# Two queues for the first four row tiles, and two inner products in rotating PSUM tiles

## The chip, the cores and the metric

The kernel runs on one core of one Trainium2 chip. The metric is the device time of one execution in microseconds. Before the change it is 921.42 us, the median of three runs (920.85 to 922.02).

## The reference

One decoder layer with three sublayers, each followed by a layer norm without weights, all in float32. x is 16 x 256 tokens of 256 channels; the context has the same shape.

```python
# 1. "attention" against fixed keys and values, 4 heads of 64
xn = layernorm(x) * ln_g + ln_b
s  = einsum('bhtd,sd->bhts', heads(xn), w_fc.reshape(-1, 64))
a  = einsum('bhts,sd->bhtd', square(relu(s)), w_proj.T.reshape(-1, 64))
x  = LN(x + (x + a))
# 2. cross attention, 16 heads of 16, with a bias from clipped differences of frac
attn = gamma * (Q @ K.T) / 4 + delta * (ap * max(D, 0) + an * min(D, 0))
x  = LN(x + softmax(attn) @ V @ Wo.T + bo)
# 3. feed forward with one of 8 experts, chosen by argmax(x @ gate_W.T + gate_b)
h  = relu(x @ wi_W.T + wi_b + lora_e(x))          # 1024 wide, lora of rank 4
x  = LN(x + h @ wo_W.T + wo_b)
```

## The kernel before

The 4,096 tokens are cut into eight blocks of 512, and each block into four row tiles of 128 tokens by 256 channels. The work has three stages, one after the other, with their edges overlapped. In the first, the fixed attention goes block by block: a block's rows are normalized, turned by TensorE, multiplied with the keys `kT` (L314), put through a relu on ACT (L322) and a square on DVE (L324), and multiplied with the values `vv` (L334). In the second, the cross attention goes through 64 groups of four heads, and the feed forward of blocks 0 to 6 is worked in between them. In the third, a tail, what is left of block six and all of block seven's feed forward are done. The order on each engine is the order in which the code is written (`manual_schedule`); nothing is reordered. Every engine takes its own queue in order: arithmetic, waits and the issues of transfers alike.

The start. Block 0 is loaded in four pieces, one for each row tile (L263), all issued by SP; then SP issues the two copies of `kT` (`load_first`, L83), one for each half of the partitions, then the whole of block 1 (L260), and then the weights of the cross attention (`load_cross`, L113: `wk`, `wv`, `wq`, then small vectors, L115 and L120). ACT issues the columns `ln_g` and `ln_b` (L70), loads its function table (L78) and issues `vv` (L84). Block 0's `begin` then takes mean and variance of each row tile on DVE as it comes (L189, L190), the inverse root by `ln` and `exp` on ACT (L198, L200) and three small steps on DVE, and normalizes; `turn_in` transposes and applies `ln_g` and `ln_b`; the scores follow.

Transfers that SP and ACT issue share eight completion semaphores, which the tile layer hands out in turn, in the order in which it takes the transfers to be issued. An issue whose semaphore was used by an earlier transfer waits on its queue until that one has landed.

The tail. `inner(half)` multiplies a block with four of the eight column tiles of `wi` (L828), one into each of the four PSUM tiles `banks[0..3]`; `lora(half)` adds the expert's product (L840) and empties the four through a relu into `hT`, banks 0 and 2 on ACT (L847), banks 1 and 3 on DVE (L851). `finish(j)` multiplies a row tile of `hT`, all eight column tiles in order, with `wof` (L858) into a rotating tile and adds the result to the rows on DVE (L871). Rotating tiles come from `tile_b` (L49): two buffers of one pool and, as every third, one of another, so three in turn. A tile is handed out again only when its last reader is done.

In the tail, block six goes: `inner(0)`, `lora(0)`, `inner(1)` (L1152), the last batch's output projection `project` (L559), `lora(1)`, `finish(0)`, `finish(1)`; then block seven's `turn` and block six's `finish(2)`. The changed lines are in these functions:

Of the kernel before, what the change touches and what calls it, by code (L numbers as in the profile page):

```python
# [9 lines left out]
FP = mybir.dt.float32  # L10
AF = mybir.ActivationFunctionType
ALU = mybir.AluOpType
AX = mybir.AxisListType

P = 128
# [6 lines left out]
def tile_decoder_layer(ctx: ExitStack, tc: tile.TileContext, a: dict, out: bass.AP):  # L22


    nc = tc.nc
# [4 lines left out]
    CC = C // P  # L30
# [9 lines left out]
    const = ctx.enter_context(tc.tile_pool(name="const", bufs=1))  # L40
# [8 lines left out]
    def tile_b():  # L49

        if turns:
            turns[0] += 1
            if turns[0] % 3 == 0:
                return psV.tile([P, 512], FP, tag="W", name="ps_b")
        return psB.tile([P, 512], FP, tag="B", name="ps_b")
# [9 lines left out]
    rev = const.tile([P, 4, E], FP, name="rev")  # L65
    for e in range(E):
        nc.gpsimd.memset(rev[:, :, e : e + 1], float(E - e))
    def columns(name, src, eng):
        t = const.tile([P, src.shape[1]], FP, name=name)
        eng.dma_start(out=t, in_=src)  # L70
        return t


    kT = const.tile([P, 4, C], FP, name="kT")
    ln_g = columns("ln_g", a["ln_g"], nc.scalar)
    ln_b = columns("ln_b", a["ln_b"], nc.scalar)

    nc.scalar.preload_act_table_set("natural_log_exp_and_others")  # L78
    vv = const.tile([P, CC, C], FP, name="vv")

    def load_first():
        for h in range(2):
            nc.sync.dma_start(out=kT[64 * h : 64 * h + 64], in_=a["kT"])  # L83
        nc.scalar.dma_start(out=vv, in_=a["vv"].rearrange("(c p) f -> p c f", p=P))  # L84


# [17 lines left out]
    wib = const.tile([P, FC], FP, name="wib")  # L104
# [3 lines left out]
    loraB = const.tile([P, F], FP, name="loraB")  # L108

    def load_cross():  # L110
        load = nc.sync.dma_start
        for t, n in ((wk, "wkT"), (wv, "wvT"), (wq, "wqT")):
            load(out=t, in_=a[n].rearrange("(c p) f -> p c f", p=P))  # L113
        for t, n in ((bq, "bq"), (bk, "bk"), (fcol, "frac_cols")):
            load(out=t, in_=a[n])  # L115
        for t, n in (
            (bo, "bo"), (apos, "alpha_pos"), (aneg, "alpha_neg"), (gamma, "gamma"),
            (delta, "delta"),
        ):
            load(out=t, in_=a[n].to_broadcast(list(t.shape)))  # L120

        wo_view = a["woT"].rearrange("(o g i d) f -> i g d o f", o=CC, g=4, i=2)
        bv_view = a["bv"].rearrange("x (o g i d) -> i g d (x o)", o=CC, g=4, i=2)
        for i in range(2):
            for g in range(4):
                rows = slice(64 * i + 16 * g, 64 * i + 16 * g + 16)
                load(out=wo[rows], in_=wo_view[i, g])
                load(out=bvc[rows], in_=bv_view[i, g])
# [92 lines left out]
    x_view = a["x"].rearrange("(b j p) c -> b p j c", j=4, p=P)  # L221

    def tile_x():
        return px.tile([P, 4, C], FP, tag="x", bufs=3, name="x")
# [11 lines left out]
    if True:  # L236
# [16 lines left out]
        class Block:  # L253
# [3 lines left out]
            def load(self):  # L257
                self.x = tile_x()
                if self.tb:
                    nc.sync.dma_start(out=self.x, in_=x_view[self.tb])  # L260
                else:
                    for j in range(4):
                        nc.sync.dma_start(out=self.x[:, j, :], in_=x_view[0, :, j, :])  # L263

            def measure(self, jj):
                for j in range(2 * jj, 2 * jj + 2):
# [120 lines left out]
    if True:  # L387

        vaug = []
        for i in range(2):  # L390
            t = const.tile([P, 2, NH, 2 * HD], FP, name=f"vaug{i}")
# [311 lines left out]
        def step(piece):  # L703
            if piece:
                next(piece, None)
# [3 lines left out]
    if True:  # L709
        out_view = out.rearrange("(b j p) c -> b p j c", j=4, p=P)  # L710

        class Block:
# [99 lines left out]
                self.umT = pm.tile([P, 512], FP, tag="umT", bufs=1, name="umT")  # L812
                nc.scalar.copy(self.umT, ps)

            def inner(self, half, gs=range(4)):
                if half == 0 and 0 in gs:
                    if self.tb == NB - 1:
                        h0 = pm.tile([P, 4, 512], FP, tag="pT", name="hT0")
                        h1 = p2.tile([P, 4, 2, S], FP, tag="neg", bufs=3, name="hT1")
                        self.hT = [h0[:, g] for g in range(4)]  # L820
                        self.hT += [h1[:, g].rearrange("p j k -> p (j k)") for g in range(4)]
                    else:
                        h = pm.tile([P, FC, 512], FP, tag="hT", bufs=1, name="hT")
                        self.hT = [h[:, f] for f in range(FC)]
                for g in gs:
                    f = 4 * half + g
                    for c in range(CC):
                        nc.tensor.matmul(  # L828
                            banks[g],
                            lhsT=wi[:, c, f * P : (f + 1) * P],  # L830
                            rhs=self.xT[:, c, :],
                            start=(c == 0),
                            stop=False,
                        )

            def lora(self, half, scalar=(0, 2)):
                for g in range(4):
                    f = 4 * half + g
                    rows = slice(ER * g, ER * g + ER)
                    nc.tensor.matmul(  # L840
                        banks[g], lhsT=loraB[rows, f * P : (f + 1) * P], rhs=self.umT[rows, :],
                        start=False, stop=True,
                    )
                for g in range(4):
                    f = 4 * half + g
                    if g in scalar:
                        nc.scalar.activation(  # L847
                            self.hT[f], banks[g], AF.Relu, bias=wib[:, f : f + 1]
                        )
                    else:  # L850
                        nc.vector.tensor_scalar(  # L851
                            self.hT[f], banks[g], wib[:, f : f + 1], 0.0, ALU.add, ALU.max
                        )

            def outer(self, j, ps):
# [37 lines left out]
    with tc.manual_schedule():  # L893
        rows_in[0].load()
        load_first()
        rows_in[1].load()
        rows_in[0].begin()
# [99 lines left out]
        banks = [psL.tile([P, 512], FP, tag=f"L{g}", name=f"ps_l{g}") for g in range(4)]  # L997
# [11 lines left out]
        six, seven = rows_out[NB - 2 :]  # L1009
# [139 lines left out]
        six.inner(0, range(3, 4))  # L1149
        six.lora(0)  # L1150
        end.divide()
        six.inner(1)  # L1152
        step(add)
        step(add)
        six.lora(1)
# [95 lines left out]
```

## Time and profile before

| | before |
|---|---|
| median of three runs | 921.42 us |
| profiled execution | 922.08 us |
| its span, first to last instruction | 920.2 us |
| TensorE busy | 897.5 us (98%), granted clock 0.997 |
| VectorE busy | 700.7 us (76%) |
| ScalarE busy | 591.9 us (64%) |
| GpSimd busy | 361.6 us (39%) |
| first matmul | 8.90 us |
| first product with `kT` | 11.07 us |

A profile is one execution on the chip, and its times are in microseconds from the span's start. PE is TensorE, PEld its weight load, DVE is VectorE, ACT is ScalarE, POOL is GpSimd, SP is the engine that only issues transfers. SPq and ACTq are the queues in which transfers are issued. A row of the timeline has the start, the duration (of all instructions merged in the row), engine, line, operation, the tile written and the tiles read, and how many instructions there are; in brackets stands how long the engine was idle before and what released it. A busy share is a mean over stages with different limits; what ends last where the change is made decides.

### The profile page before, as it was taken

Reading aid. Unit: us, or ns where it says so; the run is one execution under the profiler, and the core shown is the slowest. Engines: PE = TensorE matmul, PEld = TensorE weight load, DVE = VectorE, ACT = ScalarE, POOL = GpSimd, SP = SyncE. Lnnn points to the kernel's source line nnn. Section 1 sums busy time; section 2 is a strip of 40 time slices with the busy share of each in tenths; the row PEclk is TensorE's granted clock in tenths of the full one; section 3 lists DMA queues with packets and bytes.
Section 4 is the critical chain, followed back from the end, with each engine's and each line's share of the span. In section 5 each row is a group of like instructions: output and inputs, shape, how many; then the busy total and the mean of one; then the engine's idle time right before and its main releaser. Section 6 shows DMA issues by size and latency. Waiting matters only on the chain.

```text
span 920.2 us, 19083 instructions
## 1 busy us (share of the span) xinstructions
PE 897.5 (98%) x6910; PEld 544.7 (59%) x6910; DVE 700.7 (76%) x1972; ACT 591.9 (64%) x990; POOL 361.6 (39%) x352
## 2 busy tenths in 40 slices
PE   5999999999999999999999999999999999999997
PEld 2333333333466666668757766865875686586555
DVE  5798898988869688768777877876787777678443
ACT  4757877778689789646746765675675566566111
POOL 1102312222477567534625553462555346244010
PEclk9999999999999999999999999999999999999999
DMA  5411011100001221110111102011110201111001
GB/s 152 128 36 35 30 39 38 64 2 1 7 6 54 65 72 36 24 46 18 42 36 41 46 17 64 20 42 38 40 44 19 69 14 42 37 29 44 24 1 46
DMA packets 44190, 37.01 MB, mean 40 GB/s; under 512 B 14912, under 2 KB 40000, under 8 KB 44096
## 3 DMA queue, kind: packets, MB, share of 16 engines
q1 hardware_dynamic: 43536, 35.52, 13.9%
q8 instruction: 55, 0.90, 0.4%
q14 instruction: 39, 0.32, 0.1%
q10 hardware_dynamic: 560, 0.26, 0.1%
HBM read 21.07 MB, written 6.03 MB: 29 GB/s over the span
## 4 chain that ended last, share of the span: by engine, by line
PE 58%; ACT 2%; DVE 1%; issue 0%; ACTq 0%; DVEq 0%
PE ps_b L858 12%; PE ps_l L828 12%; PE ps_b L647 10%; PE ps_l L607 6%; PE ps_v L663 5%; PE ps_b L559 3%; PE ps_b L479 2%; PE ps_b L457 2%; PE ps_l L840 2%; PE ps_b L437 1%; ACT ps_l L598 1%; PE ps_b L747 1%; ACT pT L654 1%; PE ps_b L424 1%; PE ps_b L762 0%; ACT qT L447 0%
## 5 line engine op out<-in xcount | busy, mean ns | idle before, releaser
L586 POOL TENSOR_SCALAR neg<-dneg,aneg,delta 128x512 f32<-128x512 f32 x192 | 160.6, 848 | 250.6 <-ACT pT L654 224.3
L622 DVE CUSTOM_DVE_ANT_0 neg<-ps_l,neg 128x256 f32<-128x256 f32 x512 | 181.4, 420 | 47.0 <-PE ps_l L607 46.0
L598 ACT ACTIVATE ps_l<-dpos,apos_d 128x512 f32<-128x512 f32 x256 | 173.1, 687 | 31.7 <-DVE mx L622 29.1
L654 ACT ACTIVATE pT<-ps_b 128x512 f32<-128x512 f32 x256 | 143.4, 591 | 61.1 <-PE ps_b L647 59.5
L324 DVE TENSOR_TENSOR pr<-r 128x1024 f32<-128x1024 f32 x128 | 155.5, 1255 | 32.2 <-ACT r L322 31.9
L322 ACT ACTIVATE r<-ps_a 128x1024 f32<-128x1024 f32 x128 | 126.4, 1022 | 59.0 <-PE ps_a L314 33.4
L647 PE MATMUL ps_b<-ident,neg 128*128 128x128 f32 x1024 | 141.1, 279 | 4.9 <-ACT pT L654 4.0
L637 POOL TENSOR_TENSOR neg<-neg,mx 128x1024 f32<-128x1024 f32 x65 | 123.9, 1907 | 39.8 <-DVE mx L622 33.4
L647 PEld LDWEIGHTS ps_b<-ident,neg 128*128 128x128 f32 x1024 | 113.5, 141 | 43.3 <-issue 16.0
L314 PE MATMUL ps_a<-xnT,kT 64*64 64x512 f32 x1024 | 123.7, 598 | 0.3 <-ACT r L322 0.3
L334 PE MATMUL ps_v<-pr,vv 64*64 64x512 f32 x1024 | 123.5, 593 | 0.3
L858 PE MATMUL ps_b<-wof,hT 128*128 128x256 f32 x512 | 115.9, 381 | 0.1
L828 PE MATMUL ps_l<-xt,wi 128*128 128x512 f32 x256 | 115.0, 596 | 0.8 <-ACT hT L847 0.8
L858 PEld LDWEIGHTS ps_b<-wof,hT 128*128 128x128 f32 x512 | 96.4, 190 | 16.3 <-issue 2.3
L637 DVE TENSOR_TENSOR neg<-neg,mx 128x1024 f32<-128x1024 f32 x63 | 82.5, 1310 | 0.3
L607 PE MATMUL ps_l<-kM,qT 32*128 32x256 f32 x1024 | 78.9, 401 | 1.5 <-DMA kM<-keys 1.0
L334 PEld LDWEIGHTS ps_v<-pr,vv 64*64 64x64 f32 x1024 | 38.1, 132 | 70.7 <-issue 43.7
L349 POOL TENSOR_TENSOR xt<-xt,half 128x512 f32<-128x512 f32 x15 | 23.8, 1587 | 141.1 <-ACT half L348 141.1
L314 PEld LDWEIGHTS ps_a<-xnT,kT 64*64 64x64 f32 x1024 | 37.9, 134 | 67.9 <-issue 56.2
L828 PEld LDWEIGHTS ps_l<-xt,wi 128*128 128x128 f32 x256 | 46.7, 190 | 52.0 <-issue 46.1
L663 PE MATMUL ps_v<-pT,vaug 128*32 128x256 f32 x1024 | 70.5, 388 | 0.8 <-ACT pT L654 0.8
L851 DVE TENSOR_SCALAR hT<-ps_l,wib 128x512 f32<-128x512 f32 x44 | 30.5, 746 | 44.4 <-PE ps_l L840 44.4
(108 smaller groups left out, 977.9 us busy)
## 6 DMA issues: line engine op xcount, KB each, us to landing
cT<-in_ctxT SPq DMA_DIRECT2D x16, 256.0 KB
kM<-keys SPq DMA_DIRECT2D x128, 32.0 KB
v<-raw SPq DMA_DIRECT2D x128, 32.0 KB
invs<-rows SPq DMA_DIRECT2D x128, 32.0 KB
x<-in_x SPq DMA_DIRECT2D x7, 512.0 KB
out<-x SPq DMA_DIRECT2D x7, 512.0 KB
frow<-in_frac SPq DMA_DIRECT2D x16, 128.0 KB
wi<-in_wiT SPq DMA_DIRECT2D x1, 1024.0 KB
```

The costliest lines, as they stand in the source:

```text
L314: nc.tensor.matmul(sc[64 * k : 64 * k + 64, h, :], lhsT=kT[64 * h : 64 * h + 64, q, hf * P + 64 * k : hf * P + 64 * k + 64], rhs=self.xnT[ ...
L324: nc.vector.tensor_tensor(pr, r, r, ALU.mult)
L334: nc.tensor.matmul(self.acc[k][64 * h : 64 * h + 64, :], lhsT=vv[64 * k : 64 * k + 64, hf, 64 * q : 64 * q + 64], rhs=pr[64 * k : 64 * k + ...
L586: nc.gpsimd.tensor_scalar(self.neg[:, g], self.batch.dneg, aneg[:, h : h + 1], delta, ALU.mult, ALU.mult,)
L598: nc.scalar.activation(banks[g], self.batch.dpos.rearrange("p j k -> p (j k)"), AF.Copy, scale=apos_d[:, h : h + 1],)
L607: nc.tensor.matmul(banks[g][:, j * S : (j + 1) * S], lhsT=self.batch.qT[rows, self.o, j * P : (j + 1) * P], rhs=self.batch.kM[rows, self.i ...
L622: nc.vector.tensor_tensor_reduce(out=self.t[:, g, j, :], in0=banks[g][:, j * S : (j + 1) * S], in1=self.neg[:, g, j, :], scale=1.0, scalar ...
L637: eng.tensor_tensor(rows, rows, top.to_broadcast([P, 4, S]), ALU.subtract)
L647: nc.tensor.transpose(ps[:, k * S + j * P : k * S + (j + 1) * P], self.t[:, g, j, k * P : (k + 1) * P], ident,)
L654: nc.scalar.activation(self.pT[:, g, :], self.ps[g], AF.Exp)
L828: nc.tensor.matmul(banks[g], lhsT=wi[:, c, f * P : (f + 1) * P], rhs=self.xT[:, c, :], start=(c == 0), stop=False,)
L858: nc.tensor.matmul(ps[:, 0:C], lhsT=self.hT[f][:, j * P : (j + 1) * P], rhs=wof[:, f, :], start=(f == 0), stop=(f == FC - 1),)
```

## The change

Row tiles 0 and 2 of block 0 are issued by SP, 1 and 3 by ACT. `ln_g`, `ln_b`, the table load, both copies of `kT` and `vv` are issued by ACT, in this order, after its two row tiles; SP goes on with block 1 and the cross attention's weights.

`inner` gets an argument `own`: for the column tiles named there it takes a rotating tile in the place of its bank, and `lora` adds to and empties what `inner` used. Block six's second half is called with `own=(0, 1)`; every other call is as it was.

```diff
-    def columns(name, src, eng):
-        t = const.tile([P, src.shape[1]], FP, name=name)
-        eng.dma_start(out=t, in_=src)
-        return t
-
     kT = const.tile([P, 4, C], FP, name="kT")
-    ln_g = columns("ln_g", a["ln_g"], nc.scalar)
-    ln_b = columns("ln_b", a["ln_b"], nc.scalar)
-
-    nc.scalar.preload_act_table_set("natural_log_exp_and_others")
+    ln_g, ln_b = (const.tile([P, CC], FP, name=n) for n in ("ln_g", "ln_b"))
     vv = const.tile([P, CC, C], FP, name="vv")

     def load_first():
+        for t, n in ((ln_g, "ln_g"), (ln_b, "ln_b")):
+            nc.scalar.dma_start(out=t, in_=a[n])
+
+        nc.scalar.preload_act_table_set("natural_log_exp_and_others")
         for h in range(2):
-            nc.sync.dma_start(out=kT[64 * h : 64 * h + 64], in_=a["kT"])
+            nc.scalar.dma_start(out=kT[64 * h : 64 * h + 64], in_=a["kT"])
         nc.scalar.dma_start(out=vv, in_=a["vv"].rearrange("(c p) f -> p c f", p=P))
...
                     for j in range(4):
-                        nc.sync.dma_start(out=self.x[:, j, :], in_=x_view[0, :, j, :])
+                        eng = nc.scalar if j % 2 else nc.sync
+                        eng.dma_start(out=self.x[:, j, :], in_=x_view[0, :, j, :])
...
-            def inner(self, half, gs=range(4)):
+            def inner(self, half, gs=range(4), own=()):
+
+                if 0 in gs:
+                    self.banks = list(banks)
...
                 for g in gs:
                     f = 4 * half + g
+                    if g in own:
+                        self.banks[g] = tile_b()
                     for c in range(CC):
                         nc.tensor.matmul(
-                            banks[g],
+                            self.banks[g],
...
-                        banks[g], lhsT=loraB[rows, f * P : (f + 1) * P], rhs=self.umT[rows, :],
+                        self.banks[g], lhsT=loraB[rows, f * P : (f + 1) * P], rhs=self.umT[rows, :],
...
-                            self.hT[f], banks[g], AF.Relu, bias=wib[:, f : f + 1]
+                            self.hT[f], self.banks[g], AF.Relu, bias=wib[:, f : f + 1]
...
-                            self.hT[f], banks[g], wib[:, f : f + 1], 0.0, ALU.add, ALU.max
+                            self.hT[f], self.banks[g], wib[:, f : f + 1], 0.0, ALU.add, ALU.max
...
-        six.inner(1)
+        six.inner(1, own=(0, 1))
         step(add)
         step(add)
         six.lora(1)
```

## The prediction

> **What bounds the kernel now.** I read the page's busy table first, then TensorE's share of the steps, then the timeline of the two places that the change touches, the SP queue's own waits, and the DMA rates of the first 20 us. The busy line and the stage table (us; PE, PEld, DVE, ACT, POOL busy; clock, DMA share, GB/s):
>
> ```profile
> PE 897.5 (98%) x6910; PEld 544.7 (59%) x6910; DVE 700.7 (76%) x1972; ACT 591.9 (64%) x990; POOL 361.6 (39%) x352
> ...
> 16.00:40.00 24.00, 24.00 (x224) 8.94 (x220) 19.93 (x27) 17.09 (x23) 1.28 (x1) 1.00 0.51 147
> 40.00:100.00 60.00, 59.97 (x538) 22.67 (x530) 51.22 (x88) 40.62 (x55) 9.85 (x8) 1.00 0.09 28
> ```
>
> TensorE is full from 16 us on (24.00 of 24.00, 59.97 of 60.00). So whatever the start gains or loses reaches the end nearly one for one. The start, from the timeline (start, duration, engine, line):
>
> ```profile
> 0.74 1.81 SPq L263 DMA_DIRECT2D x<-in_x  x4
> ...
> 1.69 0.42 ACTq L84 DMA_DIRECT2D vv<-in_vv  x1
> ...
> 3.84 0.59 SPq L260 DMA_DIRECT2D x<-in_x  x1
> ...
> 4.47 0.51 SPq L113 DMA_DIRECT2D wk<-in_wkT  x1
> ...
> 6.06 0.43 DVE L189 BATCH_NORM_STATS2 st<-x 128x6 f32<-128x256 f32 x1 [0.43 <-DMA x<-in_x]
> ...
> 6.80 0.30 ACT L198 ACTIVATE ln<-mv,epst 128x4 f32<-128x4 f32 x1 [3.87 <-DVE mv L190]
> ...
> 10.86 0.33 SPq L120 DMA_DIRECT2D aneg<-in_alpha_neg  x1
> ...
> 11.07 4.32 PE L314 MATMUL ps_a<-xnT,kT 64*64 64x512 f32 x24
> ```
>
> The last of the four row tiles arrives at 6.06; its statistics free ACT's `ln` at 6.80, and 4.27 us later the first score product starts. The queue's own waits, and GB/s in 40 slices of 0.5 us from zero:
>
> ```profile
> SPq L120 <- DMA x<-in_x: 0.9, 1, 0.9
> ...
> SPq L120 <- DMA wk<-in_wkT: 0.4, 1, 0.4
> ...
> GB/s 0 0 0 68 205 266 152 324 393 387 217 295 209 191 201 309 346 373 369 371 342 269 178 80 30 7 1 23 40 64 7 64 2 66 0 66 19 47 33 33
> ```
>
> An issue can thus be held by the landing of an earlier transfer that it has nothing to do with: a small load (L120) waits for `wk`. The program as built shows why. There are eight completion semaphores, used in turn, and the ninth transfer to be issued waits until the first has landed. `aneg` waits for `wk`'s, so `wk` landed at 10.86.
>
> **The start, what moves.** Row tiles 0 and 2 stay on SP, 1 and 3 go to ACT; `ln_g`, `ln_b`, the table load, the two halves of `kT` and `vv` follow on ACT; on SP the next block's 512 KB and `wk` move up behind two row tiles. The built program's waits on ACT are then: first `kT` for row tile 1, second `kT` for row tile 2, and `vv` for `wk`. `vv` is the third queued instruction ahead of `ln`. ACT's queue runs in order, so `ln` and all that follows stand behind the landing of `wk`, which no arithmetic needs yet.
>
> *Row tiles.* Four issues in one queue took 1.81 us; two and two take half, so the last tile is issued 0.9 us sooner, and neither `vv` nor the tiny `ln` columns share its way. The bounds for the end of the statistics (6.70 before: 6.52 and 0.18): with no wait after the first tile at 2.96, four pairs of 0.56 us give 5.2; with only the issue time saved, 5.8. I take 5.4, since the best slices (393, 387) had both queues on row-sized pieces. Alone that would be 1.3 us gained.
>
> The Trainium skill ("DMA: Bandwidth & Descriptors", section "Issuing engines are not separate DMA queues") says that issuing from several engines saves only the sequencer's time. By it the statistics end at 5.8 and the gain is 0.9 instead of 1.3, if nothing holds `ln`.
>
> *The hold.* When does `wk` land? Before, what had to pass up to and with it was x 524, `vv` 262, `kT` 524, next x 524, `wk` 262 = 2096 thousand bytes. The rate line, half a microsecond a slice, sums to 1968 by 9.0 us and reaches 2096 at 9.35; it landed at 10.86, a lag of 1.5 us. After, `vv` is not ahead (it waits for `wk`). With all of `kT` ahead: 1834, reached at 8.6 in the old rate line, landing 10.1. With none of `kT` ahead: 1310, reached at 6.8, landing 8.3. The old line is slow at first (345 thousand by 3.5 us, one queue issuing); at 390 GB/s from 2.0 the four tiles would be through at 3.35 instead of 4.05, so up to 0.7 us comes off: 9.4 and 7.6. `kT` is issued only after row tile 1, about 3.2, so by the 1.0 us from first issue to first data it starts near 4.3, when most of the next block's rows still have to move; it then shares. Hence between the two, 8.6. The far ends: 6.1, if the lag were gone as well (7.6 less 1.5), and 10.1. Adding `vv`'s own issue (0.42) and 0.03 before `ln`, `ln` starts at 9.05 against 6.80: **+2.25 us** (ends -0.25 and +3.75).
>
> How the two queues share is shown by 4.0 to 4.5 us, where ACT's queue had 69.5% and SP's 41.7% of the engines' time. The skill (same page, "Queues, rings and completion order") has each DMA engine alternate between queues packet by packet. As `kT`'s pieces are the larger, by that rule nearly all of `kT` passes first, 9.4, and the sum would be +3.05.
>
> *Nothing else is late.* `kT` is needed 4.27 us after `ln`, at 13.3, and by the bound above everything up to `kT` has landed by 10.1. `vv` is issued at 8.6 and first needed at 16.6 + 2.25; 262 thousand bytes at the 200 GB/s of the slow slices take 1.3 us, with the lag 2.8. The second block's x lands sooner and is read at step 3. SP's later loads wait on the same ring of semaphores at about the old times, and none is read before the second block's steps. `ln_g`/`ln_b` are issued by 2.6 and read at 12. The table load (1.28) ends near 4, before `ln`.
>
> **The tail, block six.** Before, the second half's first product must wait until ACT has emptied bank 0 (start, duration, engine, line; idle before it):
>
> ```profile
> 855.87 1.14 PE L840 MATMUL ps_l<-umT,loraB 32*128 32x512 f32 x8
> ...
> 857.03 1.27 ACT L847 ACTIVATE hT<-ps_l,wib 128x512 f32<-128x512 f32 x2 [2.19 <-PE ps_l L840]
> ...
> 857.77 7.13 PE L828 MATMUL ps_l<-xt,wi 128*128 128x512 f32 x16 [0.76 <-ACT hT L847]
> ...
> 867.63 7.17 PE L858 MATMUL ps_b<-wof,hT 128*128 128x256 f32 x32
> 867.72 1.27 ACT L847 ACTIVATE hT<-ps_l,wib 128x512 f32<-128x512 f32 x2 [9.42 <-PE ps_l L840]
> ```
>
> Removed: 0.76 us, since two rotating tiles, last read at 846 to 851, are free; banks 2 and 3 are emptied by 858.5, before TensorE comes to them (857.0 + 2 x 1.8 = 860.6). Next in line is `project`: `oT` is ready at 862.71 and TensorE would come at about 863.6, so no stall. But the rotation has three tiles. After the two come `project` (turn_um's old tile) and then `finish(0)`, which gets the tile of the first of the two. In the built program its first product waits for the ACT relu that empties that tile. Before, it started at once (867.63) because it began with the first half's `hT`; the same relu was needed only by its fifth product, behind four others. Now lora ends at 866.94, the relu runs from 866.96 for 0.64 (half of 1.27), and TensorE resumes 0.76 after lora's end, as it did at 857.77. **-0.76 + 0.76 = 0**; ends -0.76 (no new wait) and +0.2 (relu 0.1 late, no full gain). `finish(1)` gets the other tile, emptied by DVE long before, and from there the tiles repeat as before. DVE's earlier work gains nothing: `turn` starts when `finish(1)` ends (874.6).
>
> **The sum.** Span 920.2 + 2.25 + 0 = 922.45. The profiled execution took 922.08, 1.88 around its span, and lies 0.66 above the median of 921.42. Median after: 921.42 + 2.25 = **923.7 us**. 0.2% (1.84 us) is about what a measurement of this kernel can tell from no change.
>
> **Rivals.**
> - *The start gains (not slower).* Were `wk` to land before 6.35, `ln` would not be late. With the hold gone altogether and the statistics at 5.4: 921.42 - 1.3 = 920.1, and 919.4 if the tail also keeps its 0.76. For it: `wk` is issued near 2.2 instead of 4.47. Against: 1310 thousand bytes by 6.35 less the 1.5 lag would need 460 GB/s from 2.0 on; the best slice is 393.
> - *`kT` passes first and the lag grows.* `wk` at 10.1 or a little later: +3.75, 925.2. For it: the slices with `kT` in them (5.0 to 7.5) have only 191 to 295 GB/s. Against: it starts behind the row tiles and finds the next block half moved.
> - *The tail keeps its gain.* If the relu that frees the tile came under other work: 923.7 - 0.76 = 922.9. Against: the wait stands in the built program and nothing lies between lora and `finish(0)`.
>
> **How the numbers follow.** Forecast (+0.5 to +3.3) 0.78, of which about 0.55 above 1.84 and 0.23 under it; start gains 0.09 (0.05 of it faster by over 0.2%, 0.04 within); `kT` first 0.08; tail gains 0.05 (half within). So slower 0.65, same 0.30, faster 0.05. For the forecast alone 921.9 to 924.7; with the rivals and the 0.6 us by which the shown runs differ from their median, 921.0 to 925.4.
>
> **What the profile will show.** Right: `vv`'s issue on ACT's queue near 8.6, `ln` straight behind it near 9.05 with its releaser a DMA or issue rather than `mv`; statistics done near 5.4; first score near 13.3; at the tail no gap before the half's first product, and a gap of about 0.76 with releaser ACT hT before the first product of `finish(0)`. Wrong: `ln` within 0.3 us of the last `mv`, scores before 11, or `kT`/`vv` named as what TensorE waits for.

## The result and the profile after

The changed kernel takes 924.64 us (median of 11 runs, 922.0 to 925.52) against 921.42 us before (11 runs, 919.95 to 922.42). The ratio is 1.0032, with a 95% interval of 1.0021 to 1.0043: slower by 1.9 to 4.0 us. The forecast was 923.7 in a range of 921.0 to 925.4.

Runs of one kernel differ by 1.6 to 4.4 us from the fastest to the slowest. So below, a mechanism is read from the rows of a profile and a verdict from the ratio, never from the span of a single run.

The start of the kernel after, from the timeline (start, duration, engine, line; idle before and its releaser):

```profile
0.73 0.86 SPq L260 DMA_DIRECT2D x<-in_x  x2
0.73 0.89 ACTq L260 DMA_DIRECT2D x<-in_x  x2
...
2.12 0.51 SPq L109 DMA_DIRECT2D wk<-in_wkT  x1
...
3.43 0.43 DVE L185 BATCH_NORM_STATS2 st<-x 128x6 f32<-128x256 f32 x1 [3.43 <-DMA x<-in_x]
3.60 1.17 ACTq L79 DMA_DIRECT2D kT<-in_kT  x2
...
5.05 0.40 DVE L185 BATCH_NORM_STATS2 st<-x 128x6 f32<-128x256 f32 x1
5.47 0.18 DVE L186 BATCH_NORM_AGGREGATE mv<-st 128x2 f32<-128x6 f32 x1
...
8.92 0.39 ACTq L80 DMA_DIRECT2D vv<-in_vv  x1
9.42 0.30 ACT L194 ACTIVATE ln<-mv,epst 128x4 f32<-128x4 f32 x1 [5.46 <-DMA kT<-in_kT]
...
11.36 0.33 SPq L116 DMA_DIRECT2D bo<-in_bo  x1
...
13.69 2.84 PE L311 MATMUL ps_a<-xnT,kT 64*64 64x512 f32 x12
```

The row tiles did come sooner: the statistics are done at 5.65 instead of 6.70. But ACT's arithmetic stands still for 5.46 us, from the end of the table load at 3.96 to `ln` at 9.42. The second `kT` issue on its queue is over at 4.77; the one after it, `vv`, is issued only at 8.92, and `ln` follows 0.5 us later. The first score product is at 13.69 instead of 11.07: 2.62 us late.

The releaser in the brackets is not to be taken at its word. It names `kT`, but the row at 11.36 is an SP load that waits for the semaphore of `kT`'s first half, so `kT` landed well after `ln` had started. What ended the wait is read from the semaphores: `vv` waits for `wk`'s, and in the trace that one is full at 8.90. Below, where a landing is given without a row, it is the time at which the transfer's semaphore is full in the trace.

SP's own waits after the change (us, times, longest):

```profile
SPq L116 <- DMA kT<-in_kT: 2.8, 1, 2.8
SPq L111 <- DMA ln_g<-in_ln_g: 2.6, 1, 2.6
SPq L109 <- DMA x<-in_x: 1.3, 2, 0.8
SPq L116 <- DMA wq<-in_wqT: 1.1, 1, 1.1
```

The rates of the first 20 us (GB/s in 40 slices of 0.5 us):

```profile
GB/s 0 0 0 57 129 365 381 246 230 193 255 235 296 336 340 285 231 215 205 213 171 207 207 158 162 240 125 79 7 7 6 28 25 80 7 60 21 45 45 21
```

Up to 3.5 us the two queues bring more than the one did (365 and 381 in the slices from 2.5, against 266 and 152). From 3.5 to 6.0 the rate is 193 to 255, from 6.0 to 7.5 it is 296 to 340, and from 8.0 to 11.5 it lies between 171 and 231. What each queue moved from 4.0 to 6.5 us (q1 is SP's queue, q10 ACT's; packets, MB, share of the 16 DMA engines' time):

```profile
DMA packets 838, 0.60 MB, mean 242 GB/s; under 512 B 250, under 2 KB 838, under 8 KB 838
...
q1 hardware_dynamic: 606, 0.60, 68.6%
q10 hardware_dynamic: 232, 0.00, 5.1%
```

and from 8.0 to 11.0 us:

```profile
q10 hardware_dynamic: 150, 0.40, 64.3%
q1 hardware_dynamic: 361, 0.22, 42.7%
```

A half of `kT` is 256 KB for 64 partitions, in pieces of 4 KB, and up to 6.5 us no packet of that size had moved, though the first half was issued at 3.60. ACT's queue was still at the two columns ahead of it, `ln_g` and `ln_b`, each 128 pieces of 8 bytes, while SP's queue moved 0.60 MB. The rate of these 2.5 us, 242 GB/s, is below the 369 to 373 that SP's queue reached by itself in the kernel before (8.5 to 10.0 us); whether the columns' packets cost it that isn't tested. Once `kT` moved, ACT's queue got the larger part of the bytes, 0.40 MB against 0.22.

The tail, from the chain of work that ended last, after (start, duration, what):

```profile
858.66 1.07 PE ps_l L842 x8
859.73 3.63 PE ps_b L830 x8
...
869.58 0.05 PE ps_l L842 x2
869.63 0.68 ACT hT L849
870.31 0.04 issue
870.35 7.17 PE ps_b L860 x32
```

and before:

```profile
855.94 1.11 PE ps_l L840 x8
857.05 0.68 ACT hT L847
857.73 0.04 issue
857.77 7.13 PE ps_l L828 x16
...
866.63 1.07 PE ps_l L840 x8
867.70 7.11 PE ps_b L858 x32
```

The same 0.68 us of relu on ACT, with 0.04 of issue, stands in both chains. Before, it lies between `lora(0)` and the second half's products; after, between `lora(1)` and `finish(0)`. From the start of `lora(0)` to the start of `finish(0)` it is 11.76 us in both (867.63 - 855.87 and 870.35 - 858.59).

### The profile page after: what moved, and what is told of

Its sections match the earlier page's. It is cut to its first block, busy times and chain, and to the rows that moved or that the text cites. A ratio compares the mean times of both kernels' runs of the same rounds, so it can differ in the third digit from the quotient of the medians.

```text
span 922.6 us, 19081 instructions
## 1 busy us (share of the span) xinstructions
PE 897.5 (97%) x6910; PEld 544.8 (59%) x6910; DVE 700.5 (76%) x1972; ACT 591.7 (64%) x990; POOL 361.7 (39%) x352
## 3 DMA queue, kind: packets, MB, share of 16 engines
q10 hardware_dynamic: 1008, 1.05, 0.5%
HBM read 21.07 MB, written 6.03 MB: 29 GB/s over the span
## 4 chain that ended last, share of the span: by engine, by line
PE 58%; ACT 2%; DVE 0%; issue 0%; ACTq 0%; DVEq 0%
PE ps_b L860 12%; PE ps_l L830 12%; PE ps_b L644 10%; PE ps_l L604 6%; PE ps_v L660 5%; PE ps_b L556 3%; PE ps_b L476 2%; PE ps_b L454 2%; PE ps_l L842 2%; PE ps_b L434 1%; PE ps_b L744 1%; ACT ps_l L595 1%; PE ps_b L759 1%; PE ps_b L421 1%; ACT pT L651 0%; PE ps_b L830 0%
## 5 line engine op out<-in xcount | busy, mean ns | idle before, releaser
L830 PE MATMUL ps_l<-xt,wi 128*128 128x512 f32 x248 | 111.5, 595 | 0.0
```

Of the source, the lines that this page charges most:

```text
L830: nc.tensor.matmul(self.banks[g], lhsT=wi[:, c, f * P : (f + 1) * P], rhs=self.xT[:, c, :], start=(c == 0), stop=False,)
```

## The experiments

The theory at first: ACT's `ln` is held by the issue of `vv`, which waits for `wk`; the tail's two moves cancel. The rows of the profile after added a second suspicion: `kT`, which is to be there at 13.69, landed late itself, its first half at 11.36. So two questions were asked: does each part do what was said, and what is next in line if the hold is taken away?

### The start alone

```diff
-        six.inner(1, own=(0, 1))
+        six.inner(1)
```

> The change's start alone; block six's second half uses its four banks as before. Theory (ACT's ln is held behind vv, whose issue waits until wk has landed; the tail's two moves cancel): ln starts at 9.4 (8.6 to 10.1), the first score product 4.27 us later, and the time lies 2.2 to 3.3 us above the kernel before, the same as the whole change within 0.3. Rival (part of the 3.2 us comes from the tail): clearly less than the whole change, 0.5 us or more.

Measured: ratio 1.0025 (1.0014 to 1.0036), 923.63 against 921.77. `vv` is issued at 9.46, `ln` at 9.96, the score products start at 14.23. The start alone gives the loss; the interval holds the whole change's 1.0032, so the tail's part is too small to be seen here. The ratios alone wouldn't exclude the rival's 0.5 us; the tail's rows in the next run do. The same start had its first score product at 13.69 in the change: the rows of two profiles of one start differ by half a microsecond.

### The tail alone

The start of before, with `own=(0, 1)` in the tail.

> The change's tail alone, with the start of before. Theory (the wait is moved, not removed): no gap before block six's second half, a gap of 0.76 us before the first product of finish(0), released by the relu on ACT; time as before within 0.3 us. Rival 1 (the tail keeps its gain): 0.76 us less. Rival 2 (the tail costs): 0.3 us or more above.

Measured: ratio 0.9994 (0.9984 to 1.0003), no change. Its tail in the timeline:

```profile
856.10 1.14 PE L842 MATMUL ps_l<-umT,loraB 32*128 32x512 f32 x8
...
857.17 3.70 PE L830 MATMUL ps_b<-xt,wi 128*128 128x512 f32 x8
...
867.86 7.17 PE L860 MATMUL ps_b<-wof,hT 128*128 128x256 f32 x32 [0.76 <-ACT hT L849]
```

No gap at 857.17, and one of 0.76 at 867.86, released by the relu: moved, not removed, as the theory had it. By these rows both rivals fall; the ratio alone would allow the 0.76 us of rival 1 (0.9992).

### One rotating tile in the place of two

The start of before, and

```diff
-        six.inner(1)
+        six.inner(1, own=(0,))
```

> The start of before; in the tail only the first inner product of block six's second half goes into a rotating tile. Theory (the gap of the change's tail comes from the order of the three rotating tiles): finish(0) now gets turn_um's old tile and starts at once, the second product finds bank 1 emptied (857.8 against 858.8), so both gaps of 0.76 us are gone: 0.76 us below the kernel before. Rival (bank 1 or the later tiles make a new wait of the same size): no change.

Measured: ratio 0.9988 (0.9979 to 0.9998), about 1.1 us faster.

```profile
856.78 1.14 PE L842 MATMUL ps_l<-umT,loraB 32*128 32x512 f32 x8
...
857.85 1.98 PE L830 MATMUL ps_b<-xt,wi 128*128 128x512 f32 x4
...
859.67 5.31 PE L830 MATMUL ps_l<-xt,wi 128*128 128x512 f32 x12
...
867.71 7.17 PE L860 MATMUL ps_b<-wof,hT 128*128 128x256 f32 x32
```

From `lora(0)` to `finish(0)` it is now 10.93 us instead of 11.76: no bracket, no gap. With one tile taken from the rotation of three, `finish(0)` gets `turn_um`'s old tile, long empty; with two it gets the tile that ACT is just emptying. So the second rotating tile is what cost the tail its gain.

### vv on SP: the hold taken away

```diff
-        nc.scalar.dma_start(out=vv, in_=a["vv"].rearrange("(c p) f -> p c f", p=P))
+        nc.sync.dma_start(out=vv, in_=a["vv"].rearrange("(c p) f -> p c f", p=P))
```

> The whole change, but vv is issued by SP, ahead of block 1, so that nothing on ACT's queue waits for wk. Theory A (the hold is all there is): statistics done at 5.7, ln within 0.3 us of them (it may wait to 5.2 for the second kT issue), first score product at 9.9, time 1.2 us below the kernel before. Theory B (behind the hold stands a second wait: kT on ACT's queue shares with everything on SP's queue, and its first half landed at 11.36 in the changed kernel, its second later): ln as in A, but the first score product waits for kT until 11.5 to 13, released by a transfer, time between 0.4 and 2 us above the kernel before.

Measured: ratio 1.0026 (1.0015 to 1.0037), no better than the change, and with 2.4 us (1.4 to 3.4) rather above the 0.4 to 2 of theory B.

```profile
6.12 0.30 ACT L194 ACTIVATE ln<-mv,epst 128x4 f32<-128x4 f32 x1 [2.19 <-DVE mv L186]
...
9.55 0.78 ACT L296 ACTIVATE xnT<-ps_b,ln_b,ln_g 128x512 f32<-128x512 f32 x1 [0.99 <-PE ps_b L292]
...
12.74 5.84 PE L311 MATMUL ps_a<-xnT,kT 64*64 64x512 f32 x20 [2.37 <-DMA kT<-in_kT]
...
16.20 1.02 ACT L319 ACTIVATE r<-ps_a 128x1024 f32<-128x1024 f32 x1 [5.87 <-PE ps_a L311]
```

The hold is gone: `ln` follows its statistics at 6.12, and the normalized block is ready at 10.33. But the score products wait for `kT` until 12.74, and the second half later still: the first relu of the scores starts at 16.20, against 15.74 in the change and 13.12 before. Theory A falls. Behind the hold stood a second wait, which the hold had covered. In this kernel it is longer than in the change would be: with `vv` ahead of block 1 in SP's queue, the halves of `kT` landed at 12.60 and 14.12, in the change at 11.34 and 12.88.

### wi ahead of wk: the hold taken away in another way

```diff
-        for t, n in ((wk, "wkT"), (wv, "wvT"), (wq, "wqT")):
+        for t, n in ((wi, "wiT"), (wk, "wkT"), (wv, "wvT"), (wq, "wqT")):
```

and `wi` is left out of `load_ffn`.

> The whole change, but the 1 MB load of wi is issued ahead of wk instead of behind the cross attention's loads. In the program as built the turn of the semaphores thereby shifts: vv, still on ACT's queue, now waits for row tile 2 instead of wk, and SP's queue has 1 MB more beside kT. Theory A (only the hold counts): ln at 5.7 to 6.1, first score product near 10, below the kernel before. Theory B (hold first, then kT's slow way beside SP's queue): ln at 5.7 to 6.1, but the score products wait for kT; if kT has a fixed small share of the bandwidth its halves land at 11.4 and 12.9 as in the changed kernel, if it waits for SP's queue to drain they land 2 us later or more; time 2 to 5 us above the kernel before.

Measured: ratio 1.0031 (1.0019 to 1.0042). `vv` is issued at 6.01 and `ln` starts at 6.72, later than the 5.7 to 6.1 expected, as the issue of `kT`'s second half ahead of `vv` alone took 1.58 us. ACT then waits 1.70 us for the column `ln_b`, 1 KB issued at 2.15, and the score products wait for `kT` until 13.28; the first relu of the scores is at 16.51. So `kT` again, though `vv` stayed on ACT. Its first half landed at 13.14, 1.8 us later than in the changed kernel, with 1 MB more on SP. So it has no fixed share; the columns ahead of it on ACT's queue are later too, `ln_b` by 2.75 us (10.76 against 8.01).

### kT on SP, ahead of block 1

Row tiles by two queues as in the change, `vv` on ACT, the tail as before, and

```diff
-            nc.scalar.dma_start(out=kT[64 * h : 64 * h + 64], in_=a["kT"])
+            nc.sync.dma_start(out=kT[64 * h : 64 * h + 64], in_=a["kT"])
```

> The row tiles by two queues as in the change, ln_g, ln_b, the table and vv behind them on ACT, but kT stays on SP, ahead of block 1, and the tail is as before. In the program as built vv waits for row tile 1 only. Theory B: nothing holds ln (5.6 to 6.0), kT's halves land before 9.5 since block 1 is behind them in the same queue, first score product 9.9 to 10.3; time 0.7 to 1.2 us below the kernel before. Rival (two queues for the row tiles are of no use in themselves): ln at 6.5 or later, no change.

```profile
3.83 0.39 ACTq L80 DMA_DIRECT2D vv<-in_vv  x1
...
5.97 0.30 ACT L194 ACTIVATE ln<-mv,epst 128x4 f32<-128x4 f32 x1 [2.07 <-DVE mv L186]
...
10.24 5.37 PE L311 MATMUL ps_a<-xnT,kT 64*64 64x512 f32 x32
```

Neither wait is there: the halves of `kT` landed at 6.23 and 7.73, and `ln` and the score products come 0.83 us sooner than before. The ratio, 0.9994 (0.9985 to 1.0002), agrees with 0.83 us (0.09%) but does not show it from zero. The mechanism is seen in the rows; that it shortens the kernel is not shown by this run alone.

### Both mended

The last kernel with `own=(0,)` in the tail.

> The row tiles by two queues with kT on SP, and in the tail one inner product in a rotating tile. Theory: both gains add, 0.9 and 0.8 us, 1.5 to 2.0 us below the kernel before (ratio 0.998). Rival: the start's gain is lost on the way to the end, 0.8 us alone.

Measured: ratio 0.9987 (0.9978 to 0.9996), 920.68 against 921.45. It is faster than the kernel before and so than the change. The score products start at 9.90, 1.17 us sooner than before, and from `lora(0)` to `finish(0)` it is 10.93 us, 0.83 less: both gains stand in the rows. That it is better than the one rotating tile alone (0.9988) cannot be told, so the rival, 0.8 us alone, isn't excluded by the time (1.2 us less, 0.4 to 2.0).

### A hold without a slow kT

The kernel with `kT` on SP, and six small loads ahead of `vv` on ACT, taken out of SP's later list:

```diff
+        nc.scalar.dma_start(out=bq, in_=a["bq"])
+        nc.scalar.dma_start(out=bk, in_=a["bk"])
+        nc.scalar.dma_start(out=wib, in_=a["wib"])
+        nc.scalar.dma_start(out=fcol, in_=a["frac_cols"])
+        for t, n in ((gamma, "gamma"), (delta, "delta")):
+            nc.scalar.dma_start(out=t, in_=a[n].to_broadcast(list(t.shape)))
         nc.scalar.dma_start(out=vv, in_=a["vv"].rearrange("(c p) f -> p c f", p=P))
```

> kT stays on SP ahead of block 1, the tail is as before, and vv on ACT is held on purpose: six small loads (bq, bk, wib, fcol, gamma, delta) stand ahead of it, so that the turn of the semaphores makes the last of them wait for the second half of kT (8.8 in the kernel before). So the hold is there and kT is not slow. Theory B: ACT's ln starts 0.9 to 1.2 us after the second half of kT has landed, at 9 to 10.5; the score products 4.27 us later wait for nothing else; time 2 to 3.5 us above the kernel before. Rival (ACT runs ln past issues that wait, and only kT's slow way cost the change its time): ln at 6 to 7, time as with kT on SP, 921.

```profile
5.37 0.40 DVE L187 BATCH_NORM_STATS2 st<-x 128x6 f32<-128x256 f32 x1
...
6.86 0.33 ACTq L83 DMA_DIRECT2D fcol<-in_frac_cols  x1
...
8.21 0.45 ACTq L86 DMA_DIRECT2D vv<-in_vv  x1
...
8.76 0.30 ACT L196 ACTIVATE ln<-mv,epst 128x4 f32<-128x4 f32 x1 [4.86 <-DMA fcol<-in_frac_cols]
...
13.03 4.34 PE L313 MATMUL ps_a<-xnT,kT 64*64 64x512 f32 x24
```

Measured: ratio 1.0031 (1.0020 to 1.0041). The hold came out otherwise than planned: `kT` had landed by the time its turn came, and what held the queue was `fcol`, which waits for the column `ln_g` until 6.86, and then four issues in a row. But `ln`, whose statistics are done by 6, stands behind all of them until 8.76, and the score products start 4.27 us later with no wait for `kT`. So ACT doesn't run `ln` past issues that wait, and a hold by itself delays the products by 1.96 us against before. The rival falls.

### kT on ACT with the engines to itself

`vv` on SP, the same six small loads on SP between `vv` and block 1, so that block 1 is issued at 6.47 instead of 1.64; the tail as before.

```diff
         nc.sync.dma_start(out=vv, in_=a["vv"].rearrange("(c p) f -> p c f", p=P))
+        # bq, bk, wib, fcol, gamma, delta on nc.sync, as above
```

> kT on ACT's queue as in the change, vv on SP, the tail as before, and block 1's and the weights' loads on SP come behind the same six small loads, which the turn of the semaphores holds until vv has landed, near 5.5. So kT is on ACT's queue but has the DMA engines nearly to itself. Theory (kT is slow beside SP's large loads, not by its queue): first half landed before 8, score products at 10 to 11 with no or a short wait for kT, time within 1 us of the kernel before. Rival (ACT's queue itself makes kT late): first half at 11 or later, score products at 12.5 or later, 1.5 us or more above.

```profile
6.38 0.30 ACT L196 ACTIVATE ln<-mv,epst 128x4 f32<-128x4 f32 x1 [2.45 <-DVE mv L188]
...
10.65 7.15 PE L313 MATMUL ps_a<-xnT,kT 64*64 64x512 f32 x24
...
12.48 0.31 PEld L313 LDWEIGHTS ps_a<-xnT,kT 64*64 64x64 f32 x8 [1.55 <-DMA kT<-in_kT]
```

Measured: ratio 1.0006 (0.9998 to 1.0015). `kT`'s first half, which had the engines nearly to itself, landed at 8.36 (before 8 was expected), 3.0 us sooner than in the change though it was issued a microsecond later; it is there when the normalized block is (10.60). The second half, which met block 1 on its way, makes the products wait until 12.48. So `kT` is late on ACT's queue only beside SP's large loads, and the rival falls; the time lies between, as the wait does. Whether these loads slow `kT`'s own pieces or the columns ahead of them in its queue isn't told apart: here the columns too were through sooner, `ln_b` at 5.91 against 8.01. No run has `kT` ahead of the columns on ACT.

## Why the prediction was right, and where it was off

*The hold.* Right, and the main term. It said that `wk` lands at 8.6 and `ln` starts at 9.05, +2.25 us; measured were 8.9 (from `vv`'s issue) and 9.42, +2.62. With the start alone, the same code, it was 9.46 and 9.96, +3.16, so the size was off by 0.4 to 0.9 us. That it came so near is in part luck. The rates were lower than taken: by the rate line the four tiles' 524 thousand bytes were through at about 3.74, not 3.35, and from 3.5 to 8.5 us it has 265 GB/s on the mean, where the stretch of the old line that the prediction used for the rest (4.05 to 8.64) has 285. And `kT` was to move from 4.3 on and share; nothing of it had moved by 6.5. The middle between "all of `kT` ahead" and "none" was thus too late by the order and too early by the rate, and the two errors nearly cancelled.

The Trainium skill's rule on packets ("DMA: Bandwidth & Descriptors", "Queues, rings and completion order"), as the prediction used it, would have put nearly all of `kT` ahead of `wk`. But `wk` had landed at 8.9, `kT`'s first half at 11.36. That alone doesn't speak against the rule: from 8 to 11 us, with large pieces in both queues, the queue of the larger ones did move more (0.40 MB against 0.22), though not turn by turn (150 packets against 361). What the prediction put at nothing is the time that the two columns take ahead of `kT` in its own queue.

*The row tiles.* Statistics at 5.4 foretold, 5.65 measured; the first tile came 0.47 us later than before (3.43 against 2.96), when two were loaded at once. The gain of 1.05 us is near the 0.9 that the prediction worked out from the Trainium skill ("DMA: Bandwidth & Descriptors", "Issuing engines are not separate DMA queues"), but that is no sign for it. The last row tile landed 1.74 us sooner (4.29 against 6.03), more than the 0.93 us by which its issue came sooner. That fits `vv`, which had 69.5% of the engines' time from 4.0 to 4.5 us before and no longer goes beside the row tiles; no run tests it alone. What then set the end was DVE: the four pairs follow each other without a wait from 3.43 to 5.65, as in the prediction's other bound. (The 5.4 leaned on the slices 393 and 387 as shared by both queues; in the second, 4.5 to 5.0 us, ACT's queue moved only 0.02 MB.) With `kT` on SP the gain was 0.83.

*"Nothing else is late."* Right for the changed kernel, wrong in its working. It had `kT` landed by 10.1, 3.2 us ahead of need. The first half landed at 11.36 and the second at 12.88, only 0.8 us ahead of the products; in the two kernels without the hold the products waited 2.37 and 2.30 us for its first half, and then for its second. The step that failed is the count of bytes in one line: it let two queues share as if they were one, and had `kT` start near 4.3, with the columns ahead of it, 2 KB, at no time at all.

*The first rival's price.* "With the hold gone" it gave 920.1. Two kernels without the hold took 924.2 and 924.7. Both have more on SP's queue than the change, and `kT` landed 1.3 and 1.8 us later, so they overstate the price. But with `kT` as in the change the products could not start before 11.34, still later than the 11.07 of before: by these landings an early `wk` alone would not have made the change a gain. Of the kernels tried, the two with `kT` on SP ahead of block 1 and no hold start the products soonest, at 10.24 and 9.90.

*The tail.* Right: 0.76 off one place, 0.76 on another, ratio 0.9994 for the tail alone.

*The sum.* +2.25 foretold; +3.2 in the median, with 1.9 to 4.0 as the interval, and +2.62 in the start's rows (+3.16 in those of the start alone). The 0.6 between rows and median lies inside what runs of one kernel differ by, and no run here assigns it.

## What to carry to other kernels

Before moving a transfer to an engine that also computes, write down which earlier transfer its semaphore belongs to, and which arithmetic stands behind its issue: here a load nobody needed yet stopped ACT's first arithmetic. When a wait is found, ask at once what lands next: here the two kernels without the hold gained nothing, since the keys were late too. Count also what stands ahead of a transfer in its own queue, however few bytes it has. And when a rotating buffer is lent out, count the rotation to the next user: one tile of three was free, the second was not.

## What was not expected of the hardware

Small loads are not quick beside large ones of the other queue. The 1 KB columns `ln_g` and `ln_b`, issued at 1.66 and 2.14 behind two row tiles, landed at 7.28 and 8.01 (before, issued first on ACT, at 3.10 and 3.60); SP's next small load waited 2.6 us for `ln_g`, until 7.30. With `wi` in SP's queue `ln_b` landed only at 10.8 and delayed the normalized block by 1.70 us.

And what stands behind them is late with them. `kT`'s first 256 KB, issued at 3.60 behind the columns, had moved nothing by 6.5 and took until 11.36, while 512 KB of block 1 and 256 KB of `wk` on SP passed by 8.9. From 8 to 11 us, when both queues had large pieces, ACT's queue was not the weaker one.
